# Attention scores in one ring, exponentials of two chunks at once, and a fourth expert's scores taken out by ScalarE and folded by GpSimd

## The chip, the cores and the metric

One core of one Trainium2 chip runs the whole program. The metric is the device time of one execution in microseconds; of several executions the median is taken. A core has a matrix engine (PE, with its weight loads shown apart as PEld), VectorE (DVE), ScalarE (ACT), GpSimd (POOL) and a queue engine (SP) that issues most transfers. The engines run side by side, each in the order of its own instructions, and wait for each other by semaphores.

## What is computed

Two layers over 3327 nodes of 256 features: a graph convolution and a mixture of experts, then graph attention and a block of causal attention heads. The change lies in the last block alone. It has four heads with four query experts each, over the sequence of nodes:

```python
sx = jnp.einsum('bsh,ndh->bnsd', x, hl_w) + hl_b[None, :, None, :]
pad = sx == 0
q = jnp.einsum('bnsd,neod->bneso', sx, wq)
k = jnp.einsum('bnsd,nod->bnso', sx, wk)
v = jnp.einsum('bnsd,nod->bnso', sx, wv)
scores = jnp.einsum('bnesd,bntd->bnest', q, k) * d ** 0.5 + causal
att = jax.nn.softmax(scores, axis=-1)
qkv = jnp.einsum('bnest,bntd->bnesd', att, v)
...
gs = jax.nn.softmax(jnp.einsum('bnsf,nef->bnse', out, gate_w) + gate_b[None, :, None, :], axis=-1)
mixed = jnp.einsum('bnsed,bnse->bnsd', out.reshape(b, nh, s, ne, d), gs)
```

Behind it come two normalizations, a small feed-forward step and a gate over the heads. All of it is in float32. The softmax is over at most 3327 keys, of which the causal mask leaves a row those up to itself.

## The kernel before

**Units and chunks.** The sequence is padded to 26 tiles of 128 rows. A unit is one tile `t` of queries with one head `h` of four; it holds the scores of four experts against keys up to its own tile. The keys of a unit are cut into `t // 4 + 1` chunks of up to four key tiles (`span`), so up to 512 columns: one chunk in tiles 0 to 3, two in 4 to 7, and so on to six in 20 to 23 and seven in 24 and 25. In all there are 104 units and 392 chunks, listed in `chunks` in the order of their work.

**What is done with a chunk.** `fill`: PE makes the four experts' scores into four PSUM banks (`pqk`, out of a pool `ps` of four banks that all small matmuls of the stage share). `drain`: DVE takes each bank out to SBUF (`sc`) and in the same instruction finds the row maximum, one column of `mx`; the last chunk of a unit is drained with the causal mask added. After it a small reduction gives `anmax`, the negated maximum over the unit's chunks. `weigh`: ACT takes the exponential in place, one instruction for each expert, with `anmax` as bias and the row sum into one column of `den`. `turn`: DVE transposes the chunk's four experts in 32 x 32 blocks, one instruction for all. `attend`: PE multiplies with the values (`vr`, fetched by SP), up to 128 small matmuls, and adds up in `po`. At a unit's end `over` takes `po` out (from tile 5 on by an ACT copy to `ot` and a GpSimd product with `sxd`), and one iteration later `back` turns it with four matmuls to `ptO`, which an ACT copy takes out to `qkv`.

**The order.** It is written out by hand; the wrapper `InOrder` keeps each engine's instructions in the order of the calls. The loop at the end of `heads` runs over the chunks `k`. An iteration drains the chunk that lies `2 + extra(k) + t // 4` ahead of `k` (`wanted`), attends to `k`, transposes the chunk `1 + extra(k)` ahead, takes the exponentials of the chunk `2 + extra(k)` ahead (two experts ahead of `back` and `over`, two behind; all four behind where it is the first of a unit), runs one step of the next tile's projections (`prepare`) and of up to several tails (`tail`: softmax over the gate, normalizations, feed-forward; mostly small ACT and POOL instructions), then `quiet`, which issues the ACT instructions put off in `lazy`, and last makes the scores of the next chunk. `extra` is 1 from tile 5 on while units have six chunks or fewer. So the last chunk of a unit is drained in the iteration in which the exponentials of its first chunk are issued, and the next iteration drains the next unit's first chunk and then transposes this unit's first.

**Buffers.** Score tiles come from a pool `scp` of nine buffers, 4 x 512 columns each. The projected queries of tiles 0 to 4 (`qts`) take one each of the nine until they are used up.

**Balance.** `load` adds up estimated ACT and DVE work, and `empty` gives each copy out of PSUM to the engine with less.

In the profile nearly all lines are L61, the helper that records each operation; tile names tell them apart.

Of the kernel before, what the change touches and what calls it, by code (L numbers as in the profile page):

```python
# [101 lines left out]
class Net:  # L102
# [822 lines left out]
    def heads(self, xs, vs, out):  # L925
# [3 lines left out]
        with ExitStack() as ctx:  # L929
            one = ctx.enter_context(tc.tile_pool(name="at", bufs=1))  # L930
            self.work = ctx.enter_context(tc.tile_pool(name="atw", bufs=2))
            scp = ctx.enter_context(tc.tile_pool(name="ats", bufs=9))
            vrp = ctx.enter_context(tc.tile_pool(name="atv", bufs=3))
# [8 lines left out]

            kt = one.tile([P, 4, NP], F32, name="kt")


# [31 lines left out]
            def prepare(t, res):  # L977
# [31 lines left out]
                yield  # L1009
                xt = self.work.tile([P, 2, P], F32, tag="xt", name="xt2", bufs=1)  # L1010
                turned(xn, xt)
# [8 lines left out]
                pp = self.valued(nc, partial(ps.tile, [P, 2, P], F32, tag="b", name="pv"), sxt)  # L1020
                v = self.work.tile([P, D], F32, tag="v", name="v", bufs=1)
                empty(v.rearrange("p (c q) -> p c q", c=2), pp, D)
# [3 lines left out]
            def heads_of(t, res, sxt, nz=None, v=None):  # L1026

                if nz is None:
                    nz = self.work.tile([P, 2, P], F32, tag="xn", name="nz", bufs=1)
                    nonzero(nz, sxt)  # L1030
# [18 lines left out]
                if t < AHEAD:  # L1049

                    qt = scp.tile([P, 4, BLK], F32, tag="sc", name="qts")[:, :, : 2 * P]
                    qt = qt.rearrange("p h (i q) -> p h i q", i=2)
                else:
                    qt = tl.tile([P, 4, 2, P], F32, tag="qt", name="qt")
# [16 lines left out]
            def quiet():  # L1071

                while lazy:
                    lazy.popleft()()
                for store in stores:
                    store[0] -= 1
                while stores and stores[0][0] < 0:
                    stores.popleft()[1]()
# [25 lines left out]
            def fill(u, g):  # L1104
# [5 lines left out]
                for i in range(2):  # L1110
                    pq += [ps.tile([P, BLK], F32, tag="b", name="pqk") for _ in range(2)]
                    for k in range(2):
# [4 lines left out]
                        )  # L1117

            def drain(u, g):

                n = span(u["t"], g)[1] * P
                last = g == u["t"] // 4
                if g == 0:
                    u["sc"] = {}
                    u["mx"] = sm.tile([P, 4, 8], F32, tag="mx", name="mx")
                sc = u["sc"][g] = scp.tile([P, 4, BLK], F32, tag="sc", name="sc")
                for e in range(4):
                    s, m = u["pq"][e][:, :n], u["mx"][:, e, g : g + 1]
                    if last:
                        nc.vector.tensor_tensor_reduce(  # L1130
                            sc[:, e, :n], s, mask[:, BLK - n :], 1.0, NEG, ALU.add, ALU.max, m
                        )
                    else:
                        nc.vector.tensor_scalar(
                            sc[:, e, :n], s, 1.0, None, ALU.mult, ALU.max, accum_out=m
                        )
                    load["dve"] += 0.12 + 0.00104 * n
                if last:
                    u["nmax"] = sm.tile([P, 4], F32, tag="nmax", name="anmax")
# [4 lines left out]

            def weigh(u, g, experts):

                n = span(u["t"], g)[1] * P
                q = ready[u["t"]]
                if u["h"] == g == 0 and 0 in experts:
                    q["den"] = sm.tile([P, 16, 7], F32, tag="den", name="aden", bufs=3)  # L1150
                for k in experts:
                    e = u["sc"][g][:, k, :n]
                    nc.scalar.activation(
# [12 lines left out]
            def turn(u, g):  # L1166


                n = span(u["t"], g)[1] * P
                w = u["sc"][g][:, :, :n]  # L1170
                nc.vector.transpose(w, w)
# [154 lines left out]
            def tail(t, sx, qkv, glp, den):  # L1326
# [65 lines left out]
                turned(fo, fot)  # L1392
                x = tl.tile([P, D], F32, tag="xend", name="xend", bufs=1)
                nc.sync.dma_start(out=x, in_=xs[ts(t, P), :])
# [10 lines left out]
            def last_tail(t, c, sx, r):  # L1405
# [8 lines left out]
                else:  # L1414
                    x = r["x"] = tl.tile([P, D], F32, tag="xend", name="xend", bufs=1)
                    nc.sync.dma_start(out=x, in_=xs[ts(t, P), :])
# [90 lines left out]
            units = [dict(t=t, h=h) for t in range(NT) for h in range(4)]  # L1507
            chunks = [(u, g) for u in units for g in range(u["t"] // 4 + 1)]
            def begin(u):
# [49 lines left out]
            for k in range(2):  # L1559
                values(*chunks[k])  # L1560
                weigh(*chunks[k], range(4))
            turn(*chunks[0])
            fill_next()
            ended, flipped, weighed = None, 1, 2
            for k, (u, g) in enumerate(chunks):
# [7 lines left out]
                rest = []  # L1573
                while weighed < min(k + 3 + extra(k), len(chunks)):
                    c = chunks[weighed]
                    if c[1]:
                        weigh(*c, range(2))
                    rest.append((*c, range(2 if c[1] else 0, 4)))
                    weighed += 1
                if ended:  # L1580
# [570 lines left out]
```

## Time and profile before

| | |
|---|---|
| runs: median (lowest, highest of 3) | 2846.56 us (2841.45, 2846.60) |
| the profiled execution, and its span | 2842.88 us, 2840.9 us |
| mean granted TensorE clock | 0.98 |
| first transpose of tile 0, 12, 24; last transpose | 976, 1460, 2571, 2812 us |
| score drains on DVE (plain, masked) | 1152, 416 instructions |
| exponentials on ACT | 1568 instructions, 1041.4 us busy |
| transposes on DVE | 392 instructions, 816.1 us busy |
| score matmuls on PE | 2944 records, 764.8 us busy |
| value matmuls on PE | 43728 records, 758.8 us busy |

The heads stage takes the last two thirds of the time. A row of a group view reads: line, engine, operation, what it writes and reads, shapes, count, then busy us and mean ns of one, then the idle time of the engine just before these instructions and what ended it. A row of a window view reads: the window, its length, then for PE, PEld, DVE, ACT and POOL the busy us with the count, then the granted clock, the share of the DMA engines and GB/s. A row of a timeline reads: start, length, engine, line, operation, shapes, count, and in brackets an idle time and its releaser. The time from one instruction's start to the next one's start is often less than its length, as an engine begins the next while the last results are written.

### The profile page before, as it was taken

What the parts mean: (1) busy time and instruction counts of PE and PEld (TensorE: products, weight loads), DVE (VectorE), ACT (ScalarE), POOL (GpSimd) and SP (SyncE); (2) the same over time, 40 slices, a digit from 0 to 9 for tenths busy, and PEclk for the clock granted to TensorE, in tenths of its full rate; (3) what the DMA queues carried; (4) which work ended last, traced back from release to release, by engine and by line L of the source; (5) the groups of instructions that cost most, each with busy time, mean ns of one, the idle gap of its engine ahead of it and who ended that gap; (6) DMA issues with size and microseconds to landing.
All of it is one profiled execution on the core that took longest, in us unless ns stands there. A gap on an engine that the chain in (4) does not pass through costs nothing.

```text
span 2840.9 us, 124987 instructions
## 1 busy us (share of the span) xinstructions
PE 2653.9 (93%) x53422; PEld 1970.7 (69%) x53422; DVE 2372.1 (83%) x5521; ACT 1790.9 (63%) x5131; POOL 1077.6 (38%) x1565
## 2 busy tenths in 40 slices
PE   7999988878988998999999999999999999999995
PEld 5888887756767776676666666666666666666664
DVE  5202643589999798999999999999999999999996
ACT  6520135555555467877777777777778777776774
POOL 5541644532133148655444333333233322223122
PEclk9999999989999899999999999999999999999998
DMA  9994568656785333434434443444434434444432
GB/s 379 386 339 138 191 212 281 202 188 238 277 285 174 94 91 88 117 109 112 119 108 117 118 116 114 119 120 121 115 115 116 126 116 124 123 117 117 116 106 80
DMA packets 257755, 449.29 MB, mean 158 GB/s; under 512 B 58768, under 2 KB 156176, under 8 KB 257072
## 3 DMA queue, kind: packets, MB, share of 16 engines
q1 hardware_dynamic: 245104, 417.11, 47.0%
q0 software_dynamic: 6576, 18.02, 1.7%
q8 instruction: 420, 6.88, 1.0%
q10 hardware_dynamic: 5520, 6.18, 0.6%
q14 instruction: 135, 1.11, 0.1%
HBM read 392.98 MB, written 25.88 MB: 147 GB/s over the span
## 4 chain that ended last, share of the span: by engine, by line
DVE 35%; PE 30%; ACT 4%; issue 2%; POOL 1%; DMA 0%; POOLq 0%; DVEq 0%; ACTq 0%
DVE sc L61 32%; PE pqk L61 11%; PE po L61 10%; PE acc L61 3%; ACT sc L61 2%; PE ptO L61 2%; PE pq L61 1%; PE psxt L61 1%; DVE p L61 1%; PE ph L61 0%; PE pk L61 0%; PE pt L61 0%; DVE sg L61 0%; ACT sq L61 0%; DVE u L61 0%
## 5 line engine op out<-in xcount | busy, mean ns | idle before, releaser
L61 ACT ACTIVATE sc<-sc,anmax 128x512 f32<-128x512 f32 (+3 forms) x1568 | 1041.4, 669 | 101.9 <-DVE anmax L61 101.8
L61 PEld LDWEIGHTS po<-sc,vr 32*64 32x64 f32 x43728 | 659.2, 131 | 300.9 <-issue 149.1
L61 DVE STREAM_TRANSPOSE sc<-sc 128x2048 f32<-128x2048 f32 (+3 forms) x392 | 816.1, 2082 | 11.7 <-ACT sc L61 11.5
L61 PE MATMUL po<-sc,vr 32*64 32x128 f32 x43728 | 758.8, 275 | 32.4 <-DVE sc L61 18.2
L61 PE MATMUL pqk<-kt,qt 64*128 64x512 f32 (+1 forms) x2944 | 764.8, 586 | 19.4 <-DVE fgs L61 7.1
L61 DVE TENSOR_SCALAR_CACHE_REDUCE sc<-pqk 128x512 f32<-128x512 f32 (+2 forms) x1152 | 653.3, 621 | 28.7 <-PE pqk L61 26.7
L61 PEld LDWEIGHTS pqk<-kt,qt 64*128 64x128 f32 x2944 | 315.0, 186 | 240.7 <-issue 85.5
L61 PE MATMUL acc<-wh,p 128*128 128x259 f32 x1352 | 310.9, 387 | 35.3 <-DVE p L61 35.2
L61 PEld LDWEIGHTS acc<-wh,p 128*128 128x128 f32 x1352 | 254.0, 191 | 92.2 <-DVE p L61 51.9
L61 PE MATMUL acc<-y,pan 128*128 128x256 f32 x1352 | 298.4, 382 | 1.7 <-issue 1.7
L61 ACT ACTIVATION_READ_ACCUMULATOR sc<-sc,anmax 128x1 f32 x1568 | 299.5, 191 | 0.0
L61 PEld LDWEIGHTS acc<-y,pan 128*128 128x128 f32 x1352 | 257.2, 191 | 38.7 <-issue 3.3
L61 POOL TENSOR_TENSOR ot<-ot,sxd 128x512 f32<-128x512 f32 x83 | 105.8, 1275 | 435.9 <-ACT ot L61 435.9
L61 DVE CUSTOM_DVE_ANT_0 sc<-pqk,mask 128x512 f32<-128x512 f32 (+3 forms) x416 | 242.0, 636 | 21.1 <-PE pqk L61 20.8
L61 ACT ACTIVATE u<-u,d 128x512 f32<-128x512 f32 (+1 forms) x182 | 125.1, 688 | 156.4 <-DVE u L61 156.2
L61 DVE SCALAR_TENSOR_TENSOR p<-pan,u 128x512 f32<-128x512 f32 (+1 forms) x182 | 127.7, 702 | 11.7 <-PE acc L61 7.3
L61 DVE SCALAR_TENSOR_TENSOR u<-bc,d 128x512 f32<-128x512 f32 (+1 forms) x182 | 136.3, 749 | 0.1
L61 PE MATMUL ptO<-igw,ot 128*128 128x68 f32 x832 | 116.1, 283 | 4.3 <-DVE sc L61 2.1
L61 ACT COPY qkv<-ptO 128x272 f32<-128x272 f32 x104 | 39.7, 382 | 126.7 <-PE ptO L61 126.6
L61 PEld LDWEIGHTS ptO<-igw,ot 128*128 128x128 f32 x832 | 101.8, 193 | 23.1 <-issue 15.2
L61 ACT ACTIVATE junk<-ar 128x1664 bf16<-128x1664 f32 x52 | 82.8, 1592 | 54.3 <-DMA ar<-in_adj_dram 53.7
L61 DVE CUSTOM_DVE_ANT_0 sg<-sg,dst 128x1664 bf16<-128x1664 bf16 (+2 forms) x56 | 100.7, 1806 | 1.2 <-ACT dst L61 1.0
(366 smaller groups left out, 3074.6 us busy)
## 6 DMA issues: line engine op xcount, KB each, us to landing
vr<-vs SPq DMA_DIRECT2D x976, 128.0 KB
ar<-in_adj_dram SPq DMA_DIRECT2D x104, 832.0 KB
vr<-vs SPq DMA_DIRECT2D x544, 96.0 KB
pan<-in_adjt_dram SPq DMA_DIRECT2D x156, 256.0 KB
pan<-in_adjt_dram SPq DMA_DIRECT2D x26, 1024.0 KB
pan<-in_adjt_dram SPq DMA_DIRECT2D x20, 832.0 KB
w1e<-w SPq DMA_DIRECT2D x59, 256.0 KB
took<-places SPq DMA_DIRECT2D x59, 129.0 KB
```

The costliest lines, as they stand in the source:

```text
L61: made = make(*args, **kw)
```

## The change

- Scores live in one tile `ring` of 9 x 512 columns for each expert. Chunk `c` has slot `c % 9` (`c % 6` for the first 24 chunks; the queries of tiles 0 to 4 lie in slots 6 to 8 then). A chunk with an even number in its unit that is followed by another of the same unit in the next slot is `paired`: it is put at the right end of its slot, so that the two chunks' columns adjoin.
- `weigh` takes the exponential of a pair in one ACT instruction for each expert. `den` is cleared by POOL for each tile, as a pair fills one column for two chunks. The loop hands out a pair's four experts two by two over the iterations; a pair at the head of a unit gets all four at once.
- From tile 12 on, for all chunks of a unit but its last two, ACT copies the fourth expert's scores out of PSUM in place of DVE's drain. In the next `quiet` (or later, in a drain that needs it) POOL folds the copied columns to half by an elementwise maximum in three instructions (a - b, max with 0, + b), and two drains later DVE reduces the half to the column of `mx`. The last of these reductions precedes `anmax`.
- Some buffers share others' places (`xt2` with `v`, `xend` with `xres`), and `den` has four buffers in place of three.

The program's order shows, beside this: 184 chunks with a copy and a fold (108 of 512 columns, 76 of 384), 968 exponentials in place of 1568 (of 1024 columns 212, of 896 300, of 768 72, of 640 16; the rest of one chunk each), no other instruction added, taken away or given to another engine, and the same transfers.

```diff
-            scp = ctx.enter_context(tc.tile_pool(name="ats", bufs=9))
...
+            RING = 9
+            ring = one.tile([P, 4, RING * BLK], F32, name="ring")
...
             def heads_of(t, res, sxt, nz=None, v=None):
 
+                den = sm.tile([P, 16, 7], F32, tag="den", name="aden", bufs=4)
+                nc.gpsimd.memset(den, 0.0)
+                res.update(den=den)
...
                 while lazy:
                     lazy.popleft()()
+                fold()
...
+            folds = deque()
+
+            def fold():
+
+                while folds:
+                    u, g, a, b = folds.popleft()
+                    top = tl.tile([P, BLK // 2], F32, tag="top", name="atop", bufs=2)
+                    top = u["top"][g] = top[:, : a.shape[1]]
+                    nc.gpsimd.tensor_tensor(top, a, b, ALU.subtract)
+                    nc.gpsimd.tensor_scalar(top, top, 0.0, None, ALU.max)
+                    nc.gpsimd.tensor_tensor(top, top, b, ALU.add)
+
             def drain(u, g):
 
+                c = u["c"] + g
                 n = span(u["t"], g)[1] * P
+                at = slot(c) * BLK + (BLK - n if paired(c) else 0)
                 last = g == u["t"] // 4
...
-                sc = u["sc"][g] = scp.tile([P, 4, BLK], F32, tag="sc", name="sc")
-                for e in range(4):
+                sc = u["sc"][g] = ring[:, :, ds(at, n)]
+                u["at"][g] = at
+                shared = u["t"] >= 12 and g + 2 < u["t"] // 4 + 1
+                if shared:
+                    nc.scalar.copy(sc[:, 3, :], u["pq"][3][:, :n])
+                    load["act"] += 0.14 + 0.00086 * n
+                    folds.append((u, g, sc[:, 3, : n // 2], sc[:, 3, n // 2 :]))
+                for e in range(3 if shared else 4):
...
+                if any(f[0] is u and f[1] <= g - 2 for f in folds):
+                    fold()
+                if g - 2 in u["top"]:
+                    nc.vector.tensor_reduce(
+                        u["mx"][:, 3, g - 2 : g - 1], u["top"].pop(g - 2), AX.X, ALU.max
+                    )
+                    load["dve"] += 0.35
...
-            def weigh(u, g, experts):
-
+            def slot(c):
+
+                return c % (RING if c >= 24 else 6)
+
+            def paired(c):
+
+                u, g = chunks[c]
+                return g % 2 == 0 and g < u["t"] // 4 and slot(c) + 1 == slot(c + 1)
+
+            def weigh(c, experts):
+
+                u, g = chunks[c]
                 n = span(u["t"], g)[1] * P
+                if paired(c):
+                    n += span(u["t"], g + 1)[1] * P
                 q = ready[u["t"]]
-                if u["h"] == g == 0 and 0 in experts:
-                    q["den"] = sm.tile([P, 16, 7], F32, tag="den", name="aden", bufs=3)
                 for k in experts:
-                    e = u["sc"][g][:, k, :n]
+                    e = ring[:, k, ds(u["at"][g], n)]
...
                 rest = []
-                while weighed < min(k + 3 + extra(k), len(chunks)):
-                    c = chunks[weighed]
-                    if c[1]:
-                        weigh(*c, range(2))
-                    rest.append((*c, range(2 if c[1] else 0, 4)))
-                    weighed += 1
+                until = min(k + 3 + extra(k), len(chunks))
+                while weighed < until:
+                    left = range(begun, 4)
+                    if chunks[weighed][1]:
+                        half = len(left) // 2
+                        weigh(weighed, left[:half])
+                        left = left[half:]
+                    rest.append((weighed, left))
+                    weighed += 2 if paired(weighed) else 1
+                    begun = 0
+                if weighed < len(chunks) and chunks[weighed][1] and paired(weighed) and not begun:
+                    if not rest or rest[0][1][0] > 1:
+                        weigh(weighed, range(1))
+                        rest.append((weighed, range(1, 2)))
+                        begun = 2
```

More of the change, by code (lines that the diff above doesn't have):

```diff
@@ L1009, in prepare @@
                 yield
-                xt = self.work.tile([P, 2, P], F32, tag="xt", name="xt2", bufs=1)
+                xt = self.work.tile([P, 2, P], F32, tag="v", name="xt2", bufs=1)
                 turned(xn, xt)
@@ L1020, in prepare @@
                 pp = self.valued(nc, partial(ps.tile, [P, 2, P], F32, tag="b", name="pv"), sxt)
-                v = self.work.tile([P, D], F32, tag="v", name="v", bufs=1)
+                v = self.work.tile([P, 2, P], F32, tag="v", name="v", bufs=1).rearrange("p c q -> p (c q)")
                 empty(v.rearrange("p (c q) -> p c q", c=2), pp, D)
@@ L1049, in heads_of @@
                 if t < AHEAD:
-                    qt = scp.tile([P, 4, BLK], F32, tag="sc", name="qts")[:, :, : 2 * P]
+                    qt = ring[:, :, ds(6 * BLK + 2 * P * t, 2 * P)]
                     qt = qt.rearrange("p h (i q) -> p h i q", i=2)
@@ L1117, in fill @@
                         )
+            folds = deque()
[7 more added lines that the diff above has]
+                    nc.gpsimd.tensor_tensor(top, top, b, ALU.add)
             def drain(u, g):
+                c = u["c"] + g
                 n = span(u["t"], g)[1] * P
+                at = slot(c) * BLK + (BLK - n if paired(c) else 0)
                 last = g == u["t"] // 4
                 if g == 0:
-                    u["sc"] = {}
+                    u["sc"], u["at"], u["top"] = {}, {}, {}
                     u["mx"] = sm.tile([P, 4, 8], F32, tag="mx", name="mx")
-                sc = u["sc"][g] = scp.tile([P, 4, BLK], F32, tag="sc", name="sc")
-                for e in range(4):
+                sc = u["sc"][g] = ring[:, :, ds(at, n)]
[6 more added lines that the diff above has]
+                for e in range(3 if shared else 4):
                     s, m = u["pq"][e][:, :n], u["mx"][:, e, g : g + 1]
@@ L1169, in turn @@
                 n = span(u["t"], g)[1] * P
-                w = u["sc"][g][:, :, :n]
+                w = u["sc"][g]
                 nc.vector.transpose(w, w)
@@ L1392, in tail @@
                 turned(fo, fot)
-                x = tl.tile([P, D], F32, tag="xend", name="xend", bufs=1)
+                x = tl.tile([P, D], F32, tag="xres", name="xend", bufs=2)
                 nc.sync.dma_start(out=x, in_=xs[ts(t, P), :])
@@ L1414, in last_tail @@
                 else:
-                    x = r["x"] = tl.tile([P, D], F32, tag="xend", name="xend", bufs=1)
+                    x = r["x"] = tl.tile([P, D], F32, tag="xres", name="xend", bufs=2)
                     nc.sync.dma_start(out=x, in_=xs[ts(t, P), :])
@@ L1507, in heads @@
             units = [dict(t=t, h=h) for t in range(NT) for h in range(4)]
-            chunks = [(u, g) for u in units for g in range(u["t"] // 4 + 1)]
+            chunks = []
+            for u in units:
+                u["c"] = len(chunks)
+                chunks += [(u, g) for g in range(u["t"] // 4 + 1)]
             def begin(u):
@@ L1560, in heads @@
                 values(*chunks[k])
-                weigh(*chunks[k], range(4))
+                weigh(k, range(4))
             turn(*chunks[0])
             fill_next()
-            ended, flipped, weighed = None, 1, 2
+            ended, flipped, weighed, begun = None, 1, 2, 0
             for k, (u, g) in enumerate(chunks):
```

## The prediction

> **What bounds the kernel now.** I read the page's totals and slices first, then the stretches of the heads stage, then its chain of waits, then single instructions. In the slices (40 of 71 us) VectorE (DVE) is at nine tenths or more from about 1200 us on, ScalarE (ACT) at seven, GpSimd (POOL) at two to five:
>
> ```profile
> PE 2653.9 (93%) x53422; PEld 1970.7 (69%) x53422; DVE 2372.1 (83%) x5521; ACT 1790.9 (63%) x5131; POOL 1077.6 (38%) x1565
> DVE  5202643589999798999999999999999999999996
> ACT  6520135555555467877777777777778777776774
> POOL 5541644532133148655444333333233322223122
> ```
>
> By stretch (tiles 12 to 15, 16 to 19, 20 to 23; busy us with counts behind the length):
>
> ```profile
> 1460.00:1762.10 302.10, 295.29 (x8146) 203.67 (x8134) 292.21 (x672) 222.65 (x690) 120.25 (x165) 0.99 0.41 116
> 1762.10:2130.90 368.80, 362.23 (x10302) 245.57 (x10294) 360.80 (x788) 277.82 (x879) 119.00 (x164) 1.00 0.41 118
> 2130.90:2571.10 440.20, 434.77 (x12587) 293.92 (x12578) 433.38 (x924) 332.37 (x1057) 124.79 (x172) 1.00 0.42 120
> ```
>
> The third number after the length is DVE: idle 9.9, 8.0 and 6.8 us only. PE shows as busy, but its ends are modelled. Its work I take from one group's start to the next one's (medians): four score matmuls of 512 take 1.92 us, 128 value matmuls 2.02, `ptO` 1.04. Tile 22 (23 key tiles, six chunks a unit) thus needs 4 x (5 x 1.92 + 1.49 + 5 x 2.02 + 1.57 + 1.04) = 95.2 us, and about 6 for the next tile's projections and a tail; it takes 111.2. DVE needs 4 x (20 x 0.61 + 4 x 0.48 + 5 x 2.23 + 1.70 + 0.2) = 108.7 plus 1.4. So DVE is the bound and PE has some 9% left. The chain of that window agrees, PE having a third:
>
> ```profile
> by line: DVE sc L61 57.7%; PE pqk L61 15.4%; PE po L61 14.3%; ACT sc L61 2.3%; PE ptO L61 1.9%; issue 0.9%; PE psxt L61 0.8%; PE pq L61 0.7%; PE pk L61 0.6%; DVE anmax L61 0.5%; PE pt L61 0.5%; PE ph L61 0.5%; PE pv L61 0.5%; DVE gl L61 0.4
> ```
>
> One place matters most, the start of a unit's exponentials. Timelines of DVE and of ACT:
>
> ```profile
> 2286.25 0.18 DVE L61 TENSOR_REDUCE anmax<-mx 128x4 f32<-128x24 f32 x1
> 2286.34 2.30 DVE L61 STREAM_TRANSPOSE sc<-sc 128x2048 f32<-128x2048 f32 x1
> 2288.57 0.52 DVE L61 TENSOR_SCALAR_CACHE_REDUCE sc<-pqk 128x384 f32<-128x384 f32 x1
> ...
> 2290.45 1.77 DVE L61 STREAM_TRANSPOSE sc<-sc 128x1536 f32<-128x1536 f32 x1
> ```
>
> ```profile
> 2286.46 0.61 ACT L61 ACTIVATE sc<-sc,anmax 128x384 f32<-128x384 f32 x1 [4.71 <-DVE anmax L61]
> ...
> 2288.28 0.60 ACT L61 ACTIVATE sc<-sc,anmax 128x384 f32<-128x384 f32 x1
> ...
> 2288.88 0.70 ACT L61 ACTIVATE sc<-sc,anmax 128x512 f32<-128x512 f32 x1
> ```
>
> No exponential of a unit can start before `anmax` (2286.43). The transpose of its chunk 0 comes one transpose and four drains later (2290.45). The four exponentials end at 2288.88: 1.58 us to spare.
>
> **The change part by part.** The rows used:
>
> ```profile
> L61 DVE TENSOR_SCALAR_CACHE_REDUCE sc<-pqk 128x512 f32<-128x512 f32 x592 | 370.4, 680 | 11.4 <-PE pqk L61 10.5
> L61 DVE TENSOR_REDUCE l2ns<-fo 128x4 f32<-128x256 f32 x6 | 2.3, 377 | 0.0
> L61 POOL TENSOR_TENSOR fo<-fo,fng 128x256 f32<-128x256 f32 x16 | 11.7, 730 | 1.3
> L61 POOL TENSOR_SCALAR nzf<-fx 128x256 f32<-128x256 f32 x15 | 16.3, 1087 | 0.5
> ```
>
> (1) DVE drains. From tile 12 on, 184 chunks are shared (2, 3, 4 or 5 of a unit's 4, 5, 6 or 7): 108 of 512 columns, 76 of 384. Each loses one drain, 0.61 or 0.48 us from start to start, and gains a reduction of 256 or 192 values. A reduction of 256 takes 0.38 us and the next instruction starts 0.32 after it; 0.26 for 192 by the slope between the two drains. 108 x 0.285 + 76 x 0.215 = 47 us saved; with the full durations (0.385, 0.32) it is 36, with intervals of 0.30 and 0.24 it is 51. I take -47: DVE works back to back. Where PE sets the pace the saving counts less, and so do the waits below.
>
> (2) ACT. 150 pairs leave 968 exponentials in place of 1568. An exponential takes 0.71 us for 512 columns and 0.60 for 384, so 0.28 + 0.107 per 128; each of the 600 saved is worth 0.28: -168 us. The 184 copies, like `ot<-po` at 0.48 from start to start, add about 82. ACT is not the bound, so neither counts as such; 27% idle there is the cover (277.8 of 368.8 us busy in tiles 16 to 19), and (3) to (5) say where it fails. Each copy adds a wait for PE's fourth score matmul of its chunk; behind it on ACT stand the next pair's exponentials, and DVE's transposes wait for those.
>
> (3) The first exponentials are longer. A pair of 768, 896 or 1024 columns takes 0.92, 1.03 or 1.13 us; four take 3.7, 4.1 or 4.5 where they took 2.4 or 2.8. And the transpose that waits for them comes one drain earlier, as the next unit's chunk 0 has only three. In the unit shown: 4.1 + 0.03 to start + 0.12 (the smallest distance seen from an exponential's end to its transpose) = 4.25, against 4.03 - 0.48 = 3.55: DVE waits 0.7 us. Behind the transpose stand DVE's next drains, and for their banks PE's next scores. Read so for each unit from tile 12 (a chunk 0 that the ring's end leaves unpaired waits for nothing): 28 us in all if ACT is free at each `anmax`, 47 if it is as late there as now (mean 0.2 to 0.8 us by number of chunks). I take 37, the middle, as the copies skip a unit's last two chunks but the projections' copies still fall there.
>
> (4) Later exponentials. The loop now puts two to four long ones in an iteration and, for six or seven chunks, starts pair (4, 5) ahead of the last expert of pair (2, 3). From `anmax` to that one: 4.5 + 0.48 + 2.26 + 0.48 + 2.26 + 0.48 (`ot`) + 1.13 = 11.6 us, some 0.9 more with the tails' small work, against three rounds of DVE, about 13.1. Slack was 5.5 us and is 0.6. A burst of four normalization squares is 4 x 0.46 = 1.8 us. Bounds: 0, and 1.2 us in each of the 24 units of six or seven chunks, 29.
>
> (5) The copy and the fold. A late copy keeps the fourth score bank, and PE, in order, then holds the value matmuls behind its score matmul. In chunk 2 of a unit I find the copy's end 1.3 us after the drain it replaces, within PE's 9%. On POOL a fold is 0.73 + 1.09 + 0.73 = 2.5 us, 184 of them at most 470 us on an engine that is a third busy there. A fold has two rounds (9 us) before its reduction, behind which `anmax` and the next transpose stand; ahead of it in the queue are at most `ot`'s product (1.3) and one normalization (4.2). A miss would cost DVE 2 us once a tile: 0 to 28. For (4) and (5) together 0 to 40; I take 14, nearer the low end since each has slack on average. The transposes do not slow while POOL runs: 2304 ns mean at 1200 to 1300 us (POOL 55% busy), 2306 at 2400 to 2500 (25%); so nothing for that.
>
> The Trainium skill ("GPSIMD Engine Reference", Engine selection) says to keep an elementwise max or add on VectorE, as GpSimd is about two times slower with two inputs. By that rule the drain would stay on VectorE, (1) would go, and the profiled time would stand at 2843 less what pairing does. The rows show both sides: 1.46 us for the fold's two two-input steps on POOL, beside 0.29 that DVE is spared.
>
> (6) Before tile 12 there are pairs and no sharing. In tiles 8 to 11 a pair's four exponentials need 3.7 us or more, and about 4.1 are there; read as in (3), tiles 4 to 11 lose 3 us with ACT free, 20 with ACT as late as now. But ACT has 1.1 us less to do per pair, and ACT's exponentials are 7.5% of the chain in tiles 4 to 7, so a gain of 5 is possible. I take +6.
>
> (7) The last unit, where exponentials (4 x 0.71 a chunk) outlast transposes (2.3): -2 (0 to -4). The ring holds nine chunks as the pool did; 26 clears of `den` run on POOL under the projections; nothing, or 8 us at 0.3 each if POOL were late. The renamed buffers are counted at nothing: their work is the tails' and projections', a few us in each tile's 100, and if it came late the next tile's `qt` would, with DVE idle behind it. No DMA is added or moved.
>
> **Sum:** -47 + 37 + 14 + 6 - 2 = +8. The profiled execution took 2842.9 (its span 2840.9 and 2.0 around it), so 2851; the median of the three runs is 3.7 above it. A measurement of this kernel tells 0.2% (5.7 us) from no change. On the median's footing I say 2853.
>
> **The rivals.** A, faster: the waits in (3) stay at 28, (4) to (6) at a total of 3, so -47 + 28 + 3 - 2 = -18: 2829. For it: ACT idled 4.71 us before the `anmax` shown. It decides if the DVE wait on exponentials from tile 12 stays under about 30 us. B, the same: the gains and waits meet within 5.7 us, or PE, with a third of the chain, takes over both: 2846. C, much slower: ACT, now also an emptier of banks, falls behind in each unit, copies late by over 2 us hold PE, and (3) to (5) reach 47 + 40: -36 + 87 + 6 = +57, 2900; the 25% of ACT that is idle speaks against it.
>
> **How the numbers follow.** Forecast, slower by little (2853, own range 2852 to 2872): 0.38; A 0.37; B 0.17; C 0.08. Faster 0.37, same 0.17, slower 0.46. The range of 2824 to 2882 leaves out the best corner (-32 by the bounds) and most of C.
>
> **What will show it.** Step 1: 184 reductions `mx<-atop` of 0.32 to 0.38 us, and 184 drains less. Step 2: four exponentials of a pair in 3.7 to 4.5 us. Step 3: the transposes' idle time put down to ACT's exponentials, 8 us from tile 12 today, should be 30 to 50. Steps 4 and 5: waits of drains for score matmuls (21 us today) and of reductions for POOL. If the transposes wait under 20 us, I am wrong and A is right; if ACT's copies show as PE's releaser for over 30 us, C is.

## The result, and the profile after

| | before | after |
|---|---|---|
| median (lowest to highest), 5 runs each | 2846.6 us (2841.45 to 2849.0) | 2943.9 us (2939.84 to 2952.6) |
| ratio, 95% interval | | 1.0347 (1.0329 to 1.0366) |
| the profiled execution, its span | 2842.88, 2840.9 us | 2942.3, 2940.6 us |
| mean granted TensorE clock | 0.98 | 0.975 |
| first transpose of tile 0, 12, 25 | 976, 1460, 2695 us | 977, 1476, 2790 us |

The changed kernel is slower by 3.5%, outside the forecast range of 2824 to 2882. Of the 99 us between the two profiles, 79 lie between the first transposes of tiles 12 and 25 (1235.1 to 1314.3 us), 15 in tiles 0 to 11 and 5 in the last tile.

The page's totals and slices, of the kernel after:

```profile
PE 2695.4 (92%) x53422; PEld 1979.7 (67%) x53422; DVE 2336.7 (79%) x5337; ACT 1706.3 (58%) x4115; POOL 1465.9 (50%) x2143
...
DVE  5203643689999788899988998988899999998996
ACT  6410145555555566666666666666766766665763
POOL 5531644612231267644465555555456656555452
```

DVE and ACT have less to do (35 and 85 us), POOL 388 more, and the time is longer. Look at DVE's row: eights stand where nines stood. The same stretches by windows (tiles 12 to 15, 16 to 19, 20 to 23):

```profile
1475.80:1793.10 317.30, 304.84 (x8118) 206.98 (x8117) 285.67 (x638) 206.37 (x498) 188.90 (x268) 0.98 0.40 110
1793.10:2198.60 405.50, 379.61 (x10294) 250.76 (x10290) 351.85 (x737) 268.67 (x695) 221.96 (x315) 0.97 0.38 107
2198.60:2658.40 459.80, 438.94 (x12542) 288.10 (x12547) 421.03 (x857) 314.32 (x786) 264.46 (x371) 1.00 0.41 115
```

DVE (third number after the length) is idle for 31.6, 53.7 and 38.8 us, where it was 9.9, 8.0 and 6.8. ACT is idle for a third of each stretch: that an engine is far from full says nothing of how late its single instructions come. What DVE waits for from tile 12 to 24 stands in its view of waits (us in all, times, longest), before and after:

```profile
DVE sc L61 <- PE pqk L61: 20.5, 29, 2.4
DVE sc L61 <- ACT sc L61: 0.5, 2, 0.3
```

```profile
DVE ring L61 <- PE pqk L61: 74.8, 77, 3.6
DVE ring L61 <- ACT ring L61: 37.6, 48, 1.7
DVE mx L61 <- POOL atop L61: 19.1, 15, 2.9
```

Drains wait 54 us more for PE's scores, transposes 37 more for the exponentials, reductions 19 for the folds. The chain of waits of tiles 12 to 23 no longer lies on DVE: with a share of 57.7% for DVE's line of scores in the stretch shown before, it now reads

```profile
by line: ACT ring L61 19.6%; DVE ring L61 18.4%; PE pqk L61 18.0%; PE po L61 17.2%; PE ptO L61 2.7%; issue 2.6%; POOL atop L61 2.5%; ACT sq L61 2.5%; POOL fo L61 1.9%; DVE mx L61 1.6%; PE ph L61 1.1%; POOL qkv L61 1.1%; POOL ot L61 1.0%; PO
```

No engine bounds the stage: it runs in a ring over ACT, DVE and PE, each waiting for the one before. One place shows how, a timeline with rows left out:

```profile
2012.76 2.10 PE L61 MATMUL po<-ring,vr 32*64 32x128 f32 x128
...
2014.32 0.55 DVE L61 TENSOR_SCALAR_CACHE_REDUCE ring<-pqk 128x384 f32<-128x384 f32 x1
...
2014.83 1.04 ACT L61 ACTIVATE ring<-ring,anmax 128x896 f32<-128x896 f32 x1
...
2015.99 1.78 DVE L61 STREAM_TRANSPOSE ring<-ring 128x1536 f32<-128x1536 f32 x1 [1.12 <-ACT ring L61]
...
2016.97 0.47 ACT L61 COPY ring<-pqk 128x384 f32<-128x384 f32 x1
...
2017.50 3.53 PE L61 MATMUL pqk<-kt,qt 64*128 64x512 f32 x6 [0.87 <-ACT ring L61]
...
2018.89 0.56 PEld L61 LDWEIGHTS pqk<-kt,qt 64*128 64x128 f32 x4 [1.10 <-ACT sx L61]
...
2019.36 0.69 DVE L61 TENSOR_SCALAR_CACHE_REDUCE ring<-pqk 128x512 f32<-128x512 f32 x1 [0.68 <-PE pqk L61]
...
2021.00 0.69 DVE L61 TENSOR_SCALAR_CACHE_REDUCE ring<-pqk 128x512 f32<-128x512 f32 x1 [0.94 <-PE pqk L61]
```

A unit's first pair has four long exponentials in a row, the last one at 2014.83. The transpose waits for it (1.12 us). The fourth expert's copy of the next unit's first chunk stands behind it in ACT's queue, and behind four small gate exponentials: it starts at 2016.97, although its scores were there when PE went on to the value matmuls, at 2012.76. It ends 2.6 us after the third drain (2014.32 + 0.55). PE needs that bank for the next scores and waits; DVE's next drains wait for those (0.68 and 0.94). PE's six score matmuls take 3.53 us to the end of the last here, where eight took 1.92 from start to start. Their last weight loads wait 1.10 us for another small ACT copy, of `sx`, which stands behind an exponential of 1024 columns; and the clock had been lowered, of which more at the end.

### The profile page after: what moved, and what is told of

Read it like the earlier page. It is cut to its first block, busy times and chain, and to the rows that moved or that the text cites. A ratio compares the mean times of both kernels' runs of the same rounds, so it can differ in the third digit from the quotient of the medians.

```text
span 2940.6 us, 124523 instructions
## 1 busy us (share of the span) xinstructions
PE 2695.4 (92%) x53422; PEld 1979.7 (67%) x53422; DVE 2336.7 (79%) x5337; ACT 1706.3 (58%) x4115; POOL 1465.9 (50%) x2143
## 4 chain that ended last, share of the span: by engine, by line
PE 31%; DVE 20%; ACT 15%; POOL 4%; issue 2%; DMA 1%; SPq 0%; POOLq 0%; ACTq 0%; DVEq 0%
DVE ring L61 15%; ACT ring L61 12%; PE pqk L61 12%; PE po L61 11%; PE acc L61 3%; PE ptO L61 2%; ACT sq L61 1%; POOL atop L61 1%; DVE mx L61 1%; PE ph L61 1%; POOL fo L61 1%; PE pq L61 1%; DVE p L61 1%; POOL qkv L61 0%; PE pt L61 0%
## 5 line engine op out<-in xcount | busy, mean ns | idle before, releaser
L61 ACT ACTIVATE ring<-ring,anmax 128x896 f32<-128x896 f32 (+7 forms) x968 | 876.1, 909 | 138.7 <-DVE anmax L61 138.5
L61 PEld LDWEIGHTS po<-ring,vr 32*64 32x64 f32 x43728 | 671.7, 133 | 307.5 <-issue 143.4
L61 DVE STREAM_TRANSPOSE ring<-ring 128x2048 f32<-128x2048 f32 (+3 forms) x392 | 815.6, 2081 | 70.3 <-ACT ring L61 69.8
L61 PE MATMUL pqk<-kt,qt 64*128 64x512 f32 (+1 forms) x2944 | 791.2, 589 | 52.2 <-ACT ring L61 15.4
L61 PE MATMUL po<-ring,vr 32*64 32x128 f32 x43728 | 771.4, 279 | 37.4 <-DVE ring L61 20.0
L61 DVE TENSOR_SCALAR_CACHE_REDUCE ring<-pqk 128x384 f32<-128x384 f32 (+2 forms) x968 | 552.7, 621 | 87.6 <-PE pqk L61 86.3
L61 DVE CUSTOM_DVE_ANT_0 ring<-pqk,mask 128x512 f32<-128x512 f32 (+3 forms) x416 | 241.8, 636 | 19.5 <-PE pqk L61 19.3
L61 POOL TENSOR_TENSOR atop<-ring 128x256 f32<-128x256 f32 (+1 forms) x184 | 123.9, 673 | 159.4 <-ACT ring L61 139.0
L61 ACT ACTIVATION_READ_ACCUMULATOR ring<-ring,anmax 128x1 f32 x968 | 186.1, 192 | 0.0
L61 POOL TENSOR_SCALAR atop<-atop 128x256 f32<-128x256 f32 (+1 forms) x184 | 144.3, 784 | 16.1
L61 POOL TENSOR_TENSOR atop<-atop,ring 128x256 f32<-128x256 f32 (+1 forms) x184 | 123.5, 671 | 15.4
```

The costliest lines, as they stand in the source:

```text
L61: made = make(*args, **kw)
```

## The experiments

Each result is a ratio to runs of the kernel before on the same chip, with its 95% interval; "+27 us" is the ratio less 1, times 2847. "Tiles 12 to 24" is the time from the first transpose of tile 12 to that of tile 25. Two edits come again and again and are named after this: *no sharing* and *no pairs*.

```diff
-                shared = u["t"] >= 12 and g + 2 < u["t"] // 4 + 1
+                shared = False
```

```diff
-                return g % 2 == 0 and g < u["t"] // 4 and slot(c) + 1 == slot(c + 1)
+                return False
```

### The parts alone

**The ring alone** (no sharing, no pairs).

> The ring alone: no pairs, and no chunk is shared (the fourth expert is drained by VectorE as before). Control. All theories expect the time of before, 2847 within 6 us; if it is 10 us or more above, then addressing the scores in one tile, or the six slots of the first 24 chunks, costs something that the others' readings must leave out.

Measured 0.9997 (0.9984 to 1.0010): 0. The ring, the clears of `den` and the buffers with new places cost nothing, as predicted.

**Pairs alone** (no sharing).

> Ring and pairs, no chunk shared. Theory P (pairs are the cost: VectorE waits for the long exponentials at each unit's start): slower than before by 50 us or more, transposes waiting for ScalarE about 40 us from tile 12 on. Theory C (the copies are the cost: ScalarE comes late to empty the fourth bank and PE is held): within 25 us of before. Theory T (both together: pairs use up ScalarE's slack and the copies then come late): 10 to 30 us slower here, with sharing alone not slower.

Measured 1.0198 (1.0168 to 1.0228): +56.

**Sharing alone** (no pairs).

> Ring and shared chunks, no pairs. Theory P: faster than before by 20 to 36 us, as VectorE's saving of 36 us stays and its waits stay as they were. Theory C: slower than before by 30 us or more, drains waiting for score matmuls 50 us or more. Theory T: faster by 5 to 36 us, drains waiting for score matmuls under 35 us.

Measured 1.0094 (1.0064 to 1.0125): +27. Sharing is no gain, not even by itself. 56 + 27 = 83, so 16 of the 99 come from the two together. DVE's waits with sharing alone, tiles 12 to 24:

```profile
DVE ring L61 <- PE pqk L61: 58.2, 68, 3.7
DVE mx L61 <- POOL atop L61: 18.8, 17, 2.6
DVE ring L61 <- ACT ring L61: 7.1, 15, 1.3
```

The transposes hardly wait (7.1 us), so long exponentials are not needed to spoil the gain: the drains wait for PE.

**Sharing, and all pairs but a unit's first.**

```diff
+                return g and g % 2 == 0 and g < u["t"] // 4 and slot(c) + 1 == slot(c + 1)
```

> The change, but a unit's first two chunks are never a pair (their exponentials are one for each chunk); the later pairs and the sharing stay. The prediction's term for the first exponentials (37 us) expects the transposes' wait for ScalarE to fall from 47 us to about 10 and the time by about that much, to some 2905. If the pair at the head is what makes ScalarE late for the copies too, the time falls by 60 us or more. If the copies alone are the cost, it falls by under 20.

Measured 1.0364 (1.0341 to 1.0387): +104. A miss. Without the pairs to which I had put the largest cost, nothing is won back, though those pairs alone do cost something (below). The edit does remove the wait that it was made for: ahead of the first transposes of units DVE waits 0.3 us for exponentials in tiles 12 to 24 (32.8 in the changed kernel). But the later transposes now wait 30.2 us, and the drains 35 us more than in the changed kernel:

```profile
DVE ring L61 <- PE pqk L61: 109.6, 98, 3.7
DVE ring L61 <- ACT ring L61: 30.5, 31, 2.4
```

### Sharing taken apart (no pairs in all of these)

**Leave the fourth expert in PSUM.** ACT's copy, the folds and the reductions go; the fourth expert's scores of the shared chunks are not taken out at all, so its exponentials there run, in the same number, over what the slot held before, and its weights there are not the reference's. In place of it DVE clears the fourth expert's part of `mx` once for each unit.

```diff
+                    if u["t"] >= 12:
+                        nc.vector.memset(u["mx"][:, 3, :], NEG)
...
-                    nc.scalar.copy(sc[:, 3, :], u["pq"][3][:, :n])
-                    load["act"] += 0.14 + 0.00086 * n
-                    folds.append((u, g, sc[:, 3, : n // 2], sc[:, 3, n // 2 :]))
+                    pass
...
-                if any(f[0] is u and f[1] <= g - 2 for f in folds):
-                    fold()
-                if g - 2 in u["top"]:
-                    nc.vector.tensor_reduce(
-                        u["mx"][:, 3, g - 2 : g - 1], u["top"].pop(g - 2), AX.X, ALU.max
-                    )
-                    load["dve"] += 0.35
```

> No pairs, no copy and no fold: in the 184 chunks the fourth expert's scores are not taken out of PSUM at all and do not enter its maximum (so its weights are not the reference's). VectorE has 105 us less to do than before and nothing is added on any engine but 56 small clears. If VectorE alone sets the pace, with PE's 9% to spare as the prediction says, the time falls by 80 to 105 us, to some 2755. If PE sets nearly the same pace through its four banks, it falls by under 55.

**The same with the copy.** As above, but the copy and its load stay. The scores are all there and the fourth expert's maximum leaves out the shared chunks (a softmax has the same value with any shift, but the guard against overflow is then partial).

> As the last one, but ScalarE does copy the fourth expert's scores out (they are left out of its maximum, and there is no fold and no reduction). The difference to the last one is what the copy itself costs by holding its bank: 30 to 45 us if the copy theory is right, under 12 if the bank is free in time.

Measured 0.9855 (0.9838 to 0.9871), -41, for the first and 0.9916 (0.9898 to 0.9933), -24, for the second. Now sharing alone falls into three steps: -41 for the drains gone, +17 for the copies, +51 for folds and reductions (1.0094 less 0.9916), in all +27. By the prediction's prices 184 drains are 108 x 0.61 + 76 x 0.48 = 102 us of DVE's path. Only 41 of them were time. The windows of tiles 12 to 24, of the kernel before and of the one that leaves the fourth expert in PSUM (cut at the same transposes to about 1 us):

```profile
1460.00:2695.10 1235.10, 1205.53 (x34492) 818.89 (x34476) 1207.18 (x2643) 922.85 (x2911) 392.73 (x540) 1.00 0.41 118
```

```profile
1462.00:2660.60 1198.60, 1179.02 (x34514) 800.83 (x34503) 1123.91 (x2363) 921.85 (x2912) 394.39 (x553) 1.00 0.43 122
```

DVE's busy time falls by 83 us, but its idle time rises from 28 to 75. DVE's view of waits says for what, first without the copy, then with it:

```profile
DVE ring L61 <- PE pqk L61: 61.9, 85, 2.7
DVE ring L61 <- ACT ring L61: 4.3, 10, 0.8
```

```profile
DVE ring L61 <- PE pqk L61: 66.9, 88, 2.7
DVE ring L61 <- ACT ring L61: 13.4, 23, 1.6
```

Its drains wait 62 us for PE's scores, where they waited 20.5 before, while the waits of PE's matmuls for DVE fell from 21 to 11 us, and those of its weight loads from 90 to 48: PE now sets the pace as much as DVE. (That PE shows as busy for 98% proves nothing by itself; it was 98% before too.) Of the copies' +17 a hold of the fourth bank can explain only a part: the drains wait 5 us longer for scores, but the transposes 9 us longer for exponentials, which stand behind the copies in ACT's queue, and of the 8 us that PE's matmuls wait longer for ACT only 1.0 is for a copied bank. 17 lies between the two readings of the expectation (30 or more, under 12).

In the step of +51, DVE's busy time of tiles 12 to 24 rises by 47 us and its idle time by 3: it is almost all DVE's own work.

**Copies, but no folds: DVE reduces all copied columns.**

```diff
-                    top = tl.tile([P, BLK // 2], F32, tag="top", name="atop", bufs=2)
-                    top = u["top"][g] = top[:, : a.shape[1]]
-                    nc.gpsimd.tensor_tensor(top, a, b, ALU.subtract)
-                    nc.gpsimd.tensor_scalar(top, top, 0.0, None, ALU.max)
-                    nc.gpsimd.tensor_tensor(top, top, b, ALU.add)
+                    u["top"][g] = u["sc"][g][:, 3, :]
```

> No pairs; the 184 chunks are still copied out by ScalarE, but there is no fold: two drains later VectorE reduces all 512 or 384 copied columns itself. VectorE's work is then about that of before (a reduction of some 0.6 us for a drain of 0.61). Sharing alone cost +32 us against the ring alone. If the copy holds PE's banks (theory C), this stays 20 to 45 us above before, with drains waiting for score matmuls 40 us or more. If the fold on GpSimd is what costs, it comes within 8 us of before.

Measured 1.0145 (1.0127 to 1.0162): +41, against +27 with the folds. POOL's folds are worth having if the copies are; but with POOL out of it the loss stays, so it is not POOL that makes it.

**Folds, but no copies.** DVE drains all four; POOL folds what nobody reads.

```diff
-                    nc.scalar.copy(sc[:, 3, :], u["pq"][3][:, :n])
-                    load["act"] += 0.14 + 0.00086 * n
...
-                for e in range(3 if shared else 4):
+                for e in range(4):
```

and the fold and reduction ahead of `anmax` taken out as above.

> No pairs, VectorE drains all four experts as before; GpSimd makes the same 184 folds, whose results nobody reads. If the fold costs by itself (GpSimd's queue, or its traffic beside VectorE), 8 us or more above before; if not, within 6 us of before.

Measured 1.0049 (1.0030 to 1.0068): +14. The folds cost something without a reader. One could think of the exponentials, which overwrite what a fold reads; but in this trace ACT shows no wait for POOL. PE does, for the product that makes `ot` ready for `back`, which now stands behind folds in POOL's queue:

```profile
PE ptO L61 <- POOL ot L61: 11.1, 8, 1.9
```

Before, PE's matmuls show no such wait. With sharing alone it is 7.0 us.

**Sharing of a unit's first chunk alone, and of the last shared chunk alone.**

```diff
+                shared = u["t"] >= 12 and g == 0
```

> No pairs; from tile 12 on only a unit's first chunk is shared (56 chunks), which is copied just when ScalarE has the unit before it to take exponentials of. VectorE's saving is 56 times 0.2, some 11 us at most. If the place decides (ScalarE busy there), 5 to 25 us above before; if each copy costs alike, 184 copies having cost +32, about +10; if copies cost only in number, the same as the run with the last eligible chunk.

```diff
+                shared = u["t"] >= 12 and g + 3 == u["t"] // 4 + 1
```

> No pairs; from tile 12 on only the third chunk from a unit's end is shared (56 chunks), which is copied when ScalarE has gone through most of its exponentials and soon waits for the next maximum. If the place decides, 0 to 11 us below before; if each copy costs alike, about +10, as with the first chunk.

Measured 1.0026 (1.0015 to 1.0038), +7, and 1.0011 (1.0002 to 1.0021), +3. Neither place has a gain. In the second, one shared chunk of a unit, late copies aren't the reason: by the trace's records only 1 of its 56 copies there ends over 0.7 us after the third drain of its chunk (39 of 184 with all sharing and no pairs, 81 of 184 in the changed kernel). Its drains wait for PE all the same:

```profile
DVE ring L61 <- PE pqk L61: 32.0, 42, 2.3
DVE mx L61 <- POOL atop L61: 6.3, 8, 1.3
```

**Where in a unit the time goes.** I took from the traces the time from each chunk's first drain to the next chunk's first drain, tiles 12 to 24, and summed the differences to the kernel before over three groups: a unit's first two chunks (104; mean before 4.39 us), its last two (104; 4.73 us) and those between (60; 4.55 us).

| us against before | first two | between | last two |
|---|---|---|---|
| fourth expert left in PSUM | -35 | -8 | +7 |
| copies, no maximum | -31 | +4 | +7 |
| sharing alone | -34 | +17 | +46 |
| pairs alone | +39 | +1 | +1 |
| changed kernel | +14 | +20 | +48 |

With sharing, each of the first two chunks gets 34/104 = 0.32 us shorter, not the 0.48 to 0.61 of a drain. The chunks between lose a drain too and give 8 us in all with the fourth expert left in PSUM; the last two lose 7, though nothing was added to them. The reductions come two drains later, so in the last two chunks, which still have four drains of their own, and in those between: against copies without the maximum they cost 39 and 13 us there, 0.38 us for each of the last two.

### Pairs taken apart (no sharing in all of these)

**A unit's first pair alone, and the other pairs alone.**

```diff
+                return g == 0 and g < u["t"] // 4 and slot(c) + 1 == slot(c + 1)
```

> No sharing; only a unit's first two chunks are a pair. All pairs cost +57 us against the ring alone. The prediction's term (3) expects the transposes' wait for ScalarE near 30 us from tile 12 and the time up by 30 to 45 us in all, 10 to 20 of it before tile 12. If the later pairs are the cost, it is up by under 15 us.

```diff
+                return g and g % 2 == 0 and g < u["t"] // 4 and slot(c) + 1 == slot(c + 1)
```

> No sharing; only pairs behind a unit's first two chunks (units of four chunks and more). If term (3) is right and slack covers the rest, within 10 us of before. If long exponentials further on hold up ScalarE's other work (the copies of small matmul results, two experts of the next pair ahead of the last of this one), up by 20 to 45 us, with drains waiting for score matmuls.

Measured 1.0122 (1.0104 to 1.0140), +35, and 1.0147 (1.0128 to 1.0166), +42. 35 + 42 is more than the 56 of all pairs. By the profiles most of that shortfall lies in tiles 12 to 24, where the first pairs cost 16 us, the others 35, and all of them 37. With the first pairs alone the transposes' wait for exponentials (21.0 us in tiles 12 to 24, all of it ahead of first transposes) is what (3) described, though less of it; 23 us lie in tiles 0 to 11 (15 in the changed kernel, with the same pairs there). With the others alone it is PE's view of waits (weight loads and matmuls) that shows the reason, ACT's copies of `ot` and `qkv`:

```profile
PEld po L61 <- ACT ot L61: 18.1, 10, 2.9
...
PE po L61 <- ACT ot L61: 10.3, 9, 2.1
...
PEld pqk L61 <- ACT qkv L61: 8.5, 8, 3.0
```

**The copies' place.** The copy of `ot` ahead of all exponentials of a unit's last iteration (first edit, and the half of a pair begun early put behind as well), no half begun early there (second), both, and copies of `ot` and `qkv` ahead of all exponentials (third, with no half begun early in either iteration); the first edit's order without pairs as a control.

```diff
-                        half = len(left) // 2
+                        half = 0 if g == u["t"] // 4 else len(left) // 2
...
-                if weighed < len(chunks) and chunks[weighed][1] and paired(weighed) and not begun:
+                if g < u["t"] // 4 and weighed < len(chunks) and chunks[weighed][1] and paired(weighed) and not begun:
```

```diff
-                        half = len(left) // 2
+                        half = 0 if ended or g == u["t"] // 4 else len(left) // 2
...
-                if weighed < len(chunks) and chunks[weighed][1] and paired(weighed) and not begun:
+                if g < u["t"] // 4 and not ended and weighed < len(chunks) and chunks[weighed][1] and paired(weighed) and not begun:
```

> Pairs behind a unit's first two chunks alone, no sharing (that cost +42 us), but in the iteration that ends a unit the copy of the value sums (ot) goes out on ScalarE ahead of all exponentials, not behind one or two long ones. If the late copy is what the later pairs cost, PE's wait for ot (31 us from tile 12 on, 2 to 3 before) goes and the time falls by 15 us or more. If the exponentials' own lateness costs, it falls by under 8 or rises.

> Control of the last one: ring alone, no pairs, no sharing, the same order (ot ahead of the exponentials in a unit's last iteration). Expected within 8 us of before.

> Pairs behind a unit's first two chunks alone, no sharing (that cost +42 us), but no pair is begun early in the iteration that ends a unit, so ScalarE has at most two long exponentials, not four, between the last scores' copies there. If the lump of long exponentials ahead of ScalarE's copies of ot and qkv is the cost, PE's waits for these two (31 and 17 us from tile 12 on) fall by half and the time by 15 us or more. If long exponentials cost wherever they stand, the time stays within 8 us of the run without this edit.

> The same, and ot goes out ahead of all exponentials in that iteration. If the lump is the cost, PE waits under 15 us in all for ot and qkv and the time is within 15 us of before. If not, it is still 30 us or more above.

> Pairs behind a unit's first two chunks alone, no sharing (+42 us), with both copies, of ot at a unit's end and of qkv in the next iteration, ahead of all exponentials of their iteration, and no pair begun early in either. If the long exponentials cost because these copies stand behind them, PE's waits for ot and qkv fall under 15 us in all and the time comes within 18 us of before. If it stays 25 us or more above, the rest of the cost lies elsewhere.

| | ratio (95%) | us |
|---|---|---|
| all but first pairs, as in the change | 1.0147 (1.0128 to 1.0166) | +42 |
| `ot` first | 1.0135 (1.0111 to 1.0158) | +38 |
| no half begun early | 1.0109 (1.0092 to 1.0125) | +31 |
| both | 1.0112 (1.0095 to 1.0129) | +32 |
| `ot` and `qkv` first | 1.0057 (1.0040 to 1.0074) | +16 |
| `ot` first, no pairs at all | 1.0013 (1.0002 to 1.0025) | +4 |

`ot` alone was a miss: its wait goes, but `qkv`, behind the same exponentials, takes its place (of PE's weight loads 8.5 us before, 23.4 after, in tiles 12 to 24). With both ahead, PE's waits of the same kernel read

```profile
PE po L61 <- ACT ot L61: 1.0, 2, 0.5
...
PEld po L61 <- ACT ot L61: 4.7, 5, 1.3
```

with 0.8 us for `qkv`, and 26 of the 42 us are gone. So where these pairs stand alone, the place of these copies, small and few, together with the half begun early, was most of their cost; the order of this last kernel was not run without pairs.

**All pairs, with both copies first.**

> All pairs, no sharing (+57 us), in the same order. If the copies' place is what later pairs cost, what is left is about the cost of the pair at the head alone (+35 us): 2875 to 2890. Otherwise 2895 or more.

Measured 1.0192 (1.0173 to 1.0212): +55, where all pairs had +56. A miss: with the first pairs back, the copies' place is worth nothing. The traces show that there was little left to win: with all pairs and the old order PE's matmuls waited 3.8 us for `ot` and `qkv` and its weight loads 12.7, where with the later pairs alone it was 14.1 and 26.6. Why the first pairs take this wait away is open.

## Why the prediction was wrong

The direction was the likeliest one, the size was not: +8 forecast, +99 in the profiles. In the runs' terms it is -41 + 17 + 51 for sharing, 56 for pairs, and 16 for the two together.

**(1), the step that failed.** It counted 184 drains less reductions as -47, "DVE works back to back". The runs give -41 + 51 = +10 in its place, 57 of the 91 us that the sum was off. The reduction was near its price: 102 less 47 is 55 us, and 51 came. Their durations were the upper ones of the range:

```profile
L61 DVE TENSOR_REDUCE mx<-atop 128x1 f32<-128x256 f32 x108 | 44.8, 415 | 9.7 <-POOL atop L61 9.6
L61 DVE TENSOR_REDUCE mx<-atop 128x1 f32<-128x192 f32 x76 | 26.5, 348 | 9.6 <-POOL atop L61 9.6
```

The drains were not: 102 us off DVE's path were worth 41. The prediction had PE some 9% below DVE, as a mean over tile 22. For a shared chunk alone its own prices say otherwise: DVE needs 3 x 0.61 + 2.23 = 4.06 us, PE 1.92 + 2.02 = 3.94. A tenth of a microsecond is left where it had 0.73. That a chunk with a reduction (4.39) or with all four drains (4.67) beside it doesn't give it back, since PE has four banks and can't run further ahead, is my reading of the table above, not a run; shown is that DVE's drains waited 41 us more for PE's scores once the 184 drains were gone. "Where PE sets the pace the saving counts less" was written, and not worked out.

**(2), right.** ACT's busy time fell by 84.6 us, where -168 + 82 = -86 was forecast. A pair of 896 columns takes 1037 ns:

```profile
L61 ACT ACTIVATE ring<-ring,anmax 128x896 f32<-128x896 f32 x268 | 277.5, 1037 | 100.1 <-DVE anmax L61 99.9
L61 ACT COPY ring<-pqk 128x512 f32<-128x512 f32 x108 | 62.2, 576 | 45.3 <-PE pqk L61 44.5
```

As it said, nothing of that is time. (ACT's idle share is 25% by the row that it cites, not 27.)

**(3), right as a wait, not shown as a term of the sum.** Transposes wait 37.6 us for exponentials in tiles 12 to 24, 32.8 of it ahead of units' first transposes; it was 0.5 before, and 37 were forecast from tile 12 to the end. With pairs alone, where the first transpose comes a drain later, it is 22.8. In the very unit that the prediction worked through (0.7 us forecast), by DVE's timeline:

```profile
2360.14 0.18 DVE L61 TENSOR_REDUCE anmax<-mx 128x4 f32<-128x24 f32 x1
2360.24 2.30 DVE L61 STREAM_TRANSPOSE ring<-ring 128x2048 f32<-128x2048 f32 x1
...
2364.60 1.78 DVE L61 STREAM_TRANSPOSE ring<-ring 128x1536 f32<-128x1536 f32 x1 [0.65 <-ACT ring L61]
```

But the kernel without first pairs and with all else is no faster (+104 against +99). Beside sharing, this wait of DVE's is not worth its length: its view there, shown above, has DVE waiting elsewhere, and PE's matmuls wait 12.1 us for ACT's copy of `ot` (4.3 in the changed kernel).

**(4) and (5), too small: 48 in place of 14, and above the bound of 40.** Copies cost 17 us with no pair in the kernel. Pairs alone cost 56, of which (3), (6) and (7) had forecast 41, so by subtraction 15 remain for the later exponentials (no run shows this share by itself); and 16 come from the two together. "A copy within PE's 9%" was again a mean. Long exponentials make more copies late: those over 0.7 us behind their third drain are 39 of 184 without pairs and 81 with. And the step had listed `ot` among ACT's work, and among what a fold may stand behind on POOL, without asking who waits for it: PE does. With the later pairs alone that was most of their loss, and with folds alone PE waited 11 us for POOL's product of it; in the changed kernel PE's matmuls wait 8.1 us for ACT's copies of `ot` and `qkv` and 4.0 for the product.

**(6) and (7).** Tiles 0 to 11 lost 15 us (6 forecast, bounds -5 to 20), the last tile 5 (-2 forecast, bounds -4 to 0). The ring, `den` and the shared buffers: nothing, right. (2851 on the median's footing is 2855, not 2853; that changes nothing here.)

**Rival C** had much of the mechanism, "ACT, now also an emptier of banks, falls behind in each unit, copies late by over 2 us hold PE", and its sign, PE's waits put down to ACT's copies, came: 45.7 us of weight loads and 15.4 of matmuls wait for ACT's line of the ring, and 26 of the 184 copies end over 2 us late (8 without pairs). It was given 0.08 as "the 25% of ACT that is idle speaks against it". ACT is idle for 33% now, and its idle time stands ahead of `anmax` (100 us in the group above), where nothing can start; behind it four long exponentials make a queue. C's price was too low as well: it kept -36 for the drains.

On POOL the Trainium skill ("GPSIMD Engine Reference", Engine selection) would have kept the elementwise maximum on VectorE, and so the drain. The runs agree that the drain was better left on VectorE (sharing alone +27), but not for the reason given: with the copies in place, VectorE's own reduction of all copied columns lost more than POOL's folds (+41 against +27).

**What beats both kernels** is the ring with copies, no pairs and no maximum over the copied chunks: 0.9916 (0.9898 to 0.9933), with the partial guard said above. Copies gain only if nothing comes back for them.

What stays open: why the first pairs' 35 and the others' 42 make 56, why with the first pairs there PE waits so little for the copies, and how the 16 us of pairs and sharing together split.

## What to carry to other kernels

Count a saving on the bounding engine only down to the next engine's time in the same iteration, not to its mean over a tile: here 102 us taken off were worth 41, while 51 us of small work put back elsewhere counted in full. An engine that empties another's banks must be asked for its longest queue at that moment, not for its idle share; longer instructions on it are a cost for all that stands behind them, even when its total falls. And look behind every instruction that you add or lengthen for a small one that another engine waits for: a copy behind ACT's exponentials, a product behind POOL's folds.

## What had not been expected of the hardware

The TensorE clock drops in more places. The changed kernel's windows of 3.4 us at the place shown in the first timeline, and two longer ones of equal length:

```profile
2019.10:2022.50 3.40, 3.40 (x61) 1.90 (x68) 2.20 (x5) 2.26 (x4) 3.24 (x3) 0.50 0.00 0
```

```profile
1986.00:2185.00 199.00, 187.01 (x4998) 122.10 (x5006) 171.77 (x340) 133.10 (x343) 108.58 (x150) 0.95 0.38 109
2200.00:2399.00 199.00, 190.14 (x5434) 126.28 (x5434) 182.50 (x389) 141.20 (x363) 117.61 (x168) 1.00 0.41 115
```

The first is at half clock; the long ones have 0.95 and 1.00, and the one with the lower clock has 8% fewer matmuls. By the trace's clock records some 41 us of tiles 12 to 24 are at half clock, about 10 before, 31 with pairs alone, 20 with sharing alone and 3 where the fourth expert stays in PSUM. The drop shown comes just behind waits of PE, so a part of the loss may be that a wait is paid again by a slower PE. An estimate from these numbers: 31 us more at half clock are at most some 15 us of PE's work at full clock, of the 79. Which is cause and which effect no run here tells apart.

The Trainium skill ("TensorE: Matmul & The Clock Gate", Part 1: The HAM clock gate) has the gate fall to half after an idle window of about 3.4 us. Here PE's wait ahead of the drop shown was 0.87 us by its matmuls and 1.70 by its weight loads, far less. The same page ("A second HAM failure mode: psum-queue depth-cycling") tells of a kernel whose matmuls cycled through PSUM banks, and whose clock went up and down as PE idled briefly but often; the trace here looks like that case, and no run tested it by itself.
